# The last sum of the rotary embedding in a decoder's first attention: from GpSimd to VectorE

## The chip, the core and the metric

The kernel runs on one core of a Trainium2 chip. The metric is the device time of one execution in microseconds (us). All data are float32 unless said otherwise.

## What is computed

A decoder of four layers works on a stream x of shape (4, 256, 256). Each layer has three blocks (an attention, a cross block and a feed-forward block), and after each block comes x = layernorm(x + block(x)). The edit lies in the first block of layer 0, and the second block of layer 0 runs beside it. Cut to what matters:

```python
# layer 0, attention: 16 query heads of 128, one shared key and value head
q, k, v = x @ Wq, *split(x @ Wkv)
q, k = rope(q) * 128**-0.5, rope(k)   # rope(t) = t*cos + rotate_half(t)*sin
x = layernorm(x + softmax(causal(q @ k.T)) @ v @ Wout)

# layer 0, cross block: a selective scan over ctx (4, 256, 128), gated by x
u = silu(conv4(in_proj @ ctx))        # 256 channels
delta, Bm, Cm = softplus(...), ..., ...
for t in range(256):                  # 16 states per channel
    state = state * exp(delta[t] * A) + delta[t] * u[t] * Bm[t]
    y[t] = sum(state * Cm[t])
x = layernorm(x + (y + D * u) * silu(x))
```

rotate_half exchanges the two halves of a head's 128 entries and negates one of them. The remaining ten blocks are not touched.

## The kernel before

The twelve blocks are written one after the other. The instructions of each engine are put in order when the program is built: a scheduler with its own cost model arranges them, and each engine then works through its list strictly in that order, waiting at semaphores for the others. So an edit of one line can move others. Loads are issued from SP's queue.

**The attention** is `run_mqa`. Heads stand on the 128 partitions and tokens along the rows. `keys(h)` makes the keys of two batches at once (two calls), and `queries(n)`, n from 0 to 31, makes two heads of one batch: eight matmul instructions in the records into one PSUM tile of 128x512, and then the rotation. Every such tile goes through `rotated` (line 254), 34 calls in all:

- line 259, VectorE: out = ps * cos, 128x512, with ps in PSUM (in the profile qT<-ps or kT<-ps)
- lines 260 and 261, VectorE: the two halves of t = swapped ps * sin, 64x512 each (ropet<-ps); the sign is in the table
- line 262, GpSimd: out = out + t, 128x512, everything in SBUF (qT<-qT,ropet or kT<-kT,ropet)

All VectorE tensor_tensor operations go through the helper `tt` and carry line 111 in the profile; GpSimd's go through `ptt` and carry line 123, and activations of ScalarE line 126. Groups are therefore told apart by the names of their tiles. t has two buffers (`wk`), the queries have six (`qp`), and the PSUM tile of the projections (`pm`) has one.

The loop at line 368 runs n from 0 to 31. Step n covers half of the rows of one batch for four heads, with 128 keys (n even) or 256 (n odd): `shares(n)` inverts the row sums (VectorE's reciprocal of sm) and scales the exponentials p (ScalarE); `scores(n + 1)` makes the next scores (TensorE), their negated maxima nm (VectorE, two reductions) and exponentials (ScalarE); `queries(n + 4)` prepares four steps ahead; `turn(n)` transposes p; `sums(n)` and `output(n - 1)` are the products with v and Wout.

**The scan beside it.** `K.scans.beside(2)` (line 378) adds two of 64 scan steps (4 batches, 16 states) to each step of the loop. One step of the scan (`Scans._steps`):

```python
t = wk.tile([P, 2, L], F32, name="bc", tag="bc")          # Bm and Cm of this state, by DMA
K.act(dA[:, c, 1:L], delta[...], AF.Exp, scale=negA[...])  # ScalarE, twice
K.tt(s, du[:, :, lo : lo + L], again(t[:, 0, :], DC), MUL) # VectorE, s<-du,bc
nc.vector.tensor_tensor_scan(out=s, data0=dA, data1=s)     # VectorE, s<-dA,s (cut)
K.tt(s, s, again(t[:, 1, :], DC), MUL)                     # VectorE, s<-s,bc
```

All three are 128x512. TensorE adds up the states (ssmps<-s,idz). dA has three buffers and s four. Before the first step the scan has a preparation that runs beside the first steps of the attention: four products tap = tap * in on GpSimd, convolution matmuls in four groups of eight (ssmps<-ctxp,tap) into a single PSUM bank, each group moved to u by ScalarE, then Silu over all of u, the projection xd (copied by ScalarE, written to DRAM and read back as bc), delta by Exp and Ln, and du = delta * u on GpSimd.

GpSimd also adds epsilon and takes the power -0.5 for each layer norm (rstd), and multiplies the gate of the second block (gate<-gate,u, four times).

Of the kernel before, what the change touches and what calls it, by code (L numbers as in the profile page):

```python
# [29 lines left out]
ADD, SUB, MUL, MAX, MIN = ALU.add, ALU.subtract, ALU.mult, ALU.max, ALU.min  # L30
# [175 lines left out]
def again(ap, n):  # L206

    return ap.unsqueeze(1).to_broadcast([ap.shape[0], n, ap.shape[1]])
# [23 lines left out]
def run_mqa(K, w, more):  # L232
    nc, tc = K.nc, K.tc
    with ExitStack() as ctx:
# [11 lines left out]
            out=mask, in_=mask, compare_op=ALU.is_ge, fill=NEG, base=0, pattern=[[-1, P]], channel_multiplier=1  # L246
# [7 lines left out]
        def rotated(out, ps, cos, sin):  # L254

            v = lambda ap: ap.rearrange("p (b l) -> p b l", l=L)
            half = lambda ap, lo: again(ap[lo : lo + 64, :], 2)
            t = wk.tile([P, 512], F32, name="ropet")
            K.tt(v(out), v(ps), again(cos, 2), MUL)
            K.tt(v(t[0:64, :]), v(ps[64:128, :]), half(sin, 64), MUL)  # L260
            K.tt(v(t[64:128, :]), v(ps[0:64, :]), half(sin, 0), MUL)
            K.ptt(out, out, t, ADD)

        kT = one.tile([P, B * L], F32, name="kT")
        vt = one.tile([P, NT, P], F32, name="vt")
# [1 line left out]
        def keys(h):  # L267
            ps = (psc if h == 0 else pm).tile([P, 512], F32, name="ps", tag="sc" if h == 0 else "mm")
            for c in range(DC):
                K.mm(ps, w["kv"][:, c, 0:P], K.xT[:, c, 512 * h : 512 * h + 512], c == 0, c == DC - 1)  # L270
            rotated(kT[:, 512 * h : 512 * h + 512], ps, rope[:, 2, :], rope[:, 3, :])
# [9 lines left out]
        def queries(n):  # L281

            b = n // 8
            ps = pm.tile([P, 2, L], F32, name="ps", tag="mm")
            for j in range(2):
                h = n % 8 * 2 + j
                for c in range(DC):
                    K.mm(ps[:, j, :], w["q"][:, c, h * P : (h + 1) * P], K.xT[:, c, b * L : (b + 1) * L], c == 0, c == DC - 1)
            q = qp.tile([P, 2, L], F32, name="qT")
            rotated(q.rearrange("p j l -> p (j l)"), ps.rearrange("p j l -> p (j l)"), rope[:, 0, :], rope[:, 1, :])  # L290
            qT[n] = q
# [2148 lines left out]
```

## Time and profile before

| | |
|---|---|
| Median of 3 runs | 2475.49 us (2472.06 to 2479.26) |
| Profiled execution, its time | 2469.83 us |
| Its span in the profile | 2468.1 us |
| Mean granted TensorE clock | 0.948 |
| Busy: TensorE, VectorE, ScalarE, GpSimd | 2265.7, 1457.9, 801.0, 383.2 us |
| The 32 sums qT<-qT,ropet on GpSimd | 50.2 us, mean 1569 ns |
| The 2 sums kT<-kT,ropet on GpSimd | 3.0 us, mean 1516 ns |
| The 32 products qT<-ps on VectorE | 657 to 693 ns each |
| The 68 products ropet<-ps on VectorE | 683 to 694 ns each |

The first rotation starts at 10.5 us and the last one ends at 339.3 us, so everything that the edit touches lies in the first seventh of the span. In the rows of groups, a name such as s<-du,bc is what is written and what is read; then come the shapes, the count, the busy time in us and the mean in ns, and after the second bar the idle time of the engine just before. In rows ordered by time, the first two numbers are start and duration. Rows of waits give the total, the count and the longest wait, in us. The granted clock is the share of full speed at which TensorE was allowed to run. Spans on GpSimd are rough in such profiles.

### The profile page before, as it was taken

Reading aid. Unit: us, or ns where it says so; the run is one execution under the profiler, and the core shown is the slowest. Engines: PE = TensorE matmul, PEld = TensorE weight load, DVE = VectorE, ACT = ScalarE, POOL = GpSimd, SP = SyncE. Lnnn points to the kernel's source line nnn. Section 1 sums busy time; section 2 is a strip of 40 time slices with the busy share of each in tenths; the row PEclk is TensorE's granted clock in tenths of the full one; section 3 lists DMA queues with packets and bytes.
Section 4 is the critical chain, followed back from the end, with each engine's and each line's share of the span. In section 5 each row is a group of like instructions: output and inputs, shape, how many; then the busy total and the mean of one; then the engine's idle time right before and its main releaser. Section 6 shows DMA issues by size and latency. Waiting matters only on the chain. (4 is left out here: it accounts for less than half of the span.)

```text
span 2468.1 us, 28762 instructions
## 1 busy us (share of the span) xinstructions
PE 2265.7 (92%) x10624; PEld 1521.6 (62%) x10624; DVE 1457.9 (59%) x2920; ACT 801.0 (32%) x1781; POOL 383.2 (16%) x521
## 2 busy tenths in 40 slices
PE   8889998659986999899999999999999988899997
PEld 4466664325434655536888888888776543476774
DVE  3799983788875211280455444444556677774566
ACT  4567663523441111162211111111122243343434
POOL 2221214132330322200011000100210002100001
PEclk9999997778887999999999999999988899999999
DMA  6222221322213544220222112110100002100000
GB/s 201 60 60 59 53 52 35 70 48 50 52 39 101 164 131 127 78 77 9 73 82 87 45 46 73 45 63 31 46 22 1 20 18 71 41 1 1 1 1 18
DMA packets 132836, 138.99 MB, mean 56 GB/s; under 512 B 13876, under 2 KB 120726, under 8 KB 130904
## 3 DMA queue, kind: packets, MB, share of 16 engines
q1 hardware_dynamic: 132696, 137.16, 19.1%
q8 instruction: 84, 1.38, 0.2%
q14 instruction: 56, 0.46, 0.1%
HBM read 134.27 MB, written 2.85 MB: 56 GB/s over the span
## 5 line engine op out<-in xcount | busy, mean ns | idle before, releaser
L132 PE MATMUL ps<-xw,xcT 128*128 128x256 f32 (+1 forms) x2304 | 518.9, 382 | 0.3 <-ACT YT L126 0.3
L132 PEld LDWEIGHTS ps<-xw,xcT 128*128 128x128 f32 x2304 | 430.8, 190 | 64.0 <-issue 1.9
L132 PE MATMUL sc<-kT,qT 32*128 32x256 f32 (+2 forms) x1024 | 239.1, 403 | 11.7 <-DVE qn L129 11.3
L132 PEld LDWEIGHTS sc<-kT,qT 128*128 128x128 f32 (+1 forms) x1024 | 151.7, 200 | 89.7 <-issue 53.5
L111 DVE TENSOR_TENSOR xp<-ps,xb 128x256 f32<-128x256 f32 x96 | 40.4, 421 | 229.7 <-PE ps L132 229.6
L521 DVE TENSOR_TENSOR_SCAN s<-dA,s 128x512 f32<-128x512 f32 x128 | 160.2, 1266 | 15.4 <-POOL s L123 15.3
L132 PE MATMUL ssmps<-s,idz 128*128 128x512 f32 x256 | 142.8, 664 | 24.9 <-DVE s L111 24.0
L126 ACT ACTIVATE dA<-delta,negA 128x255 f32<-128x255 f32 x256 | 116.6, 501 | 133.7 <-DVE s L521 133.6
L126 ACT ACTIVATE p<-sc,nm 128x256 f32<-128x256 f32 (+1 forms) x256 | 111.8, 444 | 101.5 <-DVE nm L129 96.3
L111 DVE TENSOR_TENSOR hT<-u,a 128x512 f32<-128x512 f32 x48 | 33.2, 691 | 186.1 <-PE u L132 186.1
L132 PE MATMUL o<-pT,vt 128*128 128x256 f32 (+1 forms) x352 | 115.0, 449 | 15.5 <-ACT pT L332 15.1
L126 ACT ACTIVATE sq<-xp 128x1024 f32<-128x1024 f32 x24 | 25.4, 1057 | 314.3 <-DVE xp L111 314.3
L129 DVE TENSOR_REDUCE qn<-sc 128x2 f32<-128x480 f32 (+1 forms) x192 | 87.1, 506 | 40.1 <-PE sc L132 38.4
L123 POOL TENSOR_TENSOR xp<-xp,rn 128x128 f32<-128x128 f32 x96 | 35.2, 403 | 476.9 <-DVE rn L1408 476.9
L126 ACT ACTIVATE e<-sT 128x512 f32<-128x512 f32 x128 | 70.2, 590 | 107.7 <-PE sT L132 106.5
L129 DVE TENSOR_REDUCE nm<-sc 128x2 f32<-128x512 f32 (+1 forms) x128 | 76.7, 612 | 45.8 <-PE sc L132 45.5
L1476 DVE TENSOR_TENSOR_SCAN dec<-xT,idz 128x256 f32<-128x256 f32 (+1 forms) x192 | 89.8, 536 | 22.1 <-DMA xT<-ad 22.1
L132 PE MATMUL sT<-q,kT 32*128 32x256 f32 (+1 forms) x384 | 98.7, 501 | 1.7 <-ACT e L126 1.5
L169 POOL TENSOR_SCALAR rstd<-mv 128x2 f32<-128x2 f32 x48 | 11.7, 245 | 555.1 <-DVE mv L161 545.2
L126 ACT ACTIVATE a<-g 128x512 f32<-128x512 f32 x48 | 28.7, 597 | 206.9 <-PE g L132 206.8
L132 PE MATMUL g<-xT,wj 128*128 128x512 f32 x192 | 92.1, 603 | 0.7 <-ACT rows L100 0.7
L123 POOL TENSOR_TENSOR hT<-hT,sel 128x512 f32<-128x512 f32 x48 | 60.7, 1267 | 202.1 <-DVE hT L111 101.1
(504 smaller groups left out, 4133.2 us busy)
## 6 DMA issues: line engine op xcount, KB each, us to landing
bc<-bcd SPq DMA_DIRECT2D x128, 256.0 KB, 4.6
xw<-in_l2a_xw_dram SPq DMA_DIRECT2D x24, 768.0 KB, 4.9
xT<-ad SPq DMA_DIRECT2D x12, 1024.0 KB, 4.6
wj<-in_l1f_gate_dram SPq DMA_DIRECT2D x48, 128.0 KB, 2.5
wj<-in_l1f_up_dram SPq DMA_DIRECT2D x48, 128.0 KB, 2.8
wj<-in_l1f_down_dram SPq DMA_DIRECT2D x48, 128.0 KB, 2.9
sel<-cwd SPq DMA_DIRECT2D x32, 192.0 KB, 3.1
sel<-cwd SPq DMA_DIRECT2D x32, 128.0 KB, 3.2
```

The costliest lines, as they stand in the source:

```text
L111: self.nc.vector.tensor_tensor(out=out, in0=a, in1=b, op=op)
L123: self.nc.gpsimd.tensor_tensor(out=out, in0=a, in1=b, op=op)
L126: self.nc.scalar.activation(out, in_, func, **kw)
L129: self.nc.vector.tensor_reduce(out=out, in_=in_, axis=AX.X, op=op, **kw)
L132: self.nc.tensor.matmul(out, lhsT=lhsT, rhs=rhs, start=start, stop=stop)
L169: self.nc.gpsimd.tensor_scalar(out=out, in0=in_, scalar1=add, scalar2=None, op0=ADD)
L521: nc.vector.tensor_tensor_scan(out=s.rearrange("p c l -> p (c l)"), data0=dA.rearrange("p c l -> p (c l)"), data1=s.rearrange("p c l -> p ...
L1476: nc.vector.tensor_tensor_scan(out=dec[:, k, h, :], data0=ap[:, h, at(bb, k, j) : at(bb, k, 2)], data1=K.idz[:, 0 : (2 - j) * P], initial=0.0,
```

## The change

The fourth operation of the rotation is issued on VectorE instead of GpSimd. Its operands and its place in the source are the same; 34 instructions of 128x512 change their engine.

```diff
@@ rotated(out, ps, cos, sin)
             K.tt(v(out), v(ps), again(cos, 2), MUL)
             K.tt(v(t[0:64, :]), v(ps[64:128, :]), half(sin, 64), MUL)
             K.tt(v(t[64:128, :]), v(ps[0:64, :]), half(sin, 0), MUL)
-            K.ptt(out, out, t, ADD)
+            K.tt(out, out, t, ADD)
```

In the built program the order of the instructions changes on VectorE, ScalarE, TensorE and GpSimd within the first attention; behind it, it agrees with the order before. The order of the DMA issues on SP's queue is the same.

## The prediction

> **What bounds the kernel now.** I read the slices of the span first, for the stage in which the edited line runs: the first attention, from the start to about 370 us, with the first state-space scan beside it.
>
> ```profile
> DVE  3799983788875211280455444444556677774566
> POOL 2221214132330322200011000100210002100001
> ```
>
> One digit is 61.7 us. VectorE's second to sixth digits, 7 9 9 9 8, cover 62 to 370 us: it is full there, while GpSimd never passes a quarter. Busy times by stretch say where that begins and ends:
>
> ```profile
> core 0: us, PE busy (x) PEld busy (x) DVE busy (x) ACT busy (x) POOL busy (x), PEclk, DMA share, GB/s
> 0.00:85.00 85.00, 71.79 (x263) 43.29 (x264) 32.76 (x53) 42.55 (x97) 21.57 (x34) 0.98 0.50 158
> 85.00:100.00 15.00, 9.24 (x28) 4.79 (x27) 14.69 (x19) 6.49 (x14) 0.24 (x1) 0.97 0.26 71
> 100.00:340.00 240.00, 217.63 (x941) 152.25 (x940) 232.58 (x352) 158.64 (x457) 51.20 (x40) 0.98 0.23 58
> ```
>
> From 85 us, where the scan's first multiply runs, to 340 us VectorE is 97% busy. TensorE shows 91%, but that counts matmuls that stand in the pipeline: eight 256-column query matmuls take 1.89 us of path and are booked at 389 ns each, 3.1 us. VectorE's own waits in 100 to 340 us come to 5.8 us:
>
> ```profile
> DVE x L117 <- POOL rstd L123: 4.8, 6, 0.8
> DVE qT L111 <- PE ps L132: 1.0, 1, 1.0
> ```
>
> So in these 255 us the end is set by the sum of VectorE's instructions, and what an instruction occupies counts even when no wait is shown. Last, VectorE's groups with shapes kept apart, and the order in time (start, duration, engine, line, operation) of VectorE and GpSimd round one of the 34 rotations:
>
> ```profile
> L521 DVE TENSOR_TENSOR_SCAN s<-dA,s 128x512 f32<-128x512 f32 x51 | 64.5, 1290 | 0.0
> L111 DVE TENSOR_TENSOR s<-du,bc 128x512 f32<-128x512 f32 x52 | 53.7, 1066 | 0.1
> L111 DVE TENSOR_TENSOR s<-s,bc 128x512 f32<-128x512 f32 x50 | 32.5, 675 | 0.3
> ```
>
> ```profile
> 203.78 1.26 DVE L111 TENSOR_TENSOR s<-s,bc 128x512 f32<-128x512 f32 x2
> ...
> 208.34 0.18 DVE L320 RECIPROCAL sm<-sm 128x4 f32<-128x4 f32 x1
> 208.44 2.34 DVE L111 TENSOR_TENSOR s<-du,bc 128x512 f32<-128x512 f32 x2
> 210.70 2.33 DVE L521 TENSOR_TENSOR_SCAN s<-dA,s 128x512 f32<-128x512 f32 x2
> ```
>
> ```profile
> 208.46 1.77 POOL L123 TENSOR_TENSOR qT<-qT,ropet 128x512 f32<-128x512 f32 x1 [7.40 <-PE ps L330]
> ```
>
> Two multiplies of the same shape, both with two inputs in SBUF, take 1.26 us at 203.78 (the next starts 1.19 us later) and 2.34 us at 208.44, while GpSimd's rotation sum runs from 208.46 to 210.23. The trace has the pair as 0.66 and 1.76 us: the second stands still until GpSimd is done. GpSimd pays too: its sum takes 1.26 us alone and 1.77 us here. The mean of 1066 against 675 ns is this stall. GpSimd's "idle" 80% hides that each of its sums is paid for by VectorE.
>
> **The change, part by part.**
>
> *Removed: the stall.* Of the 34 sums, 25 run after 100 us (one of the keys, 24 of queries). For each I compared the VectorE instruction under it with the same instruction undisturbed (s<-du,bc 0.67 us, scan 1.21): 18 cost 1.00 to 1.10 us on a multiply, four 1.08 to 1.09 on a scan (2.29 us), three 0.38 to 0.41, because two instructions on PSUM filled most of the sum's time. Together 25.0 us, all on the path. The nine sums before 100 us lie under rotations and reductions that read PSUM and stall nothing (ropet 0.69 us with and without GpSimd).
>
> *A rule behind this row.* The Trainium skill ("SBUF — State Buffer", Who interferes with whom) says that a VectorE instruction with two SBUF inputs and a GpSimd instruction that reads SBUF exclude each other, the later one blocking until the earlier is through. By the rule alone each sum could cost 1.26 us, 31.5 in all; the trace has 25.0, since sums partly lie under work that doesn't contend. I take 25.0. The rule that speaks against the change is in "Perfetto Trace Analysis", Optimizing Scalar/DVE Operations: when VectorE is saturated, giving work to another engine, even GpSimd, may pay (it adds that between these two it might not). Taken plainly, 25 sums on a full engine are 15.0 us lost, 2490 us; by the row the same sums are 25.0 us lost where they are now, so the difference is a gain of 10.0.
>
> *Added: 34 sums on VectorE.* Nearest row: s<-s,bc, same shape and two SBUF inputs, 0.60 us from start to start. 25 x 0.60 = 15.0 us on the path. The upper bound is the full duration, 0.69 us (17.3), if the next instruction has to wait for the result; the built order of the changed program puts another instruction between nearly always. The nine early sums fall where VectorE is busy 39% and cost nothing: cover is idle time of up to 10.5 us before its reductions; without it, 9 x 0.60 = 5.4.
>
> *Moved: the order on VectorE.* The order is the scheduler's, so I read the built program. The two scan steps of an iteration, paired now (multiply twice, scan twice, multiply twice), are mostly interleaved with the sum and with the next maxima. One thing costs: the reciprocal of the row sums waits for ScalarE's exponentials. Now the query rotation, 2.07 us, stands between the second maximum and the reciprocal; in four iterations of the saturated stage there is only one 0.60 us multiply there. ScalarE needs 1.2 to 1.35 us after the second maximum (206.24 to 207.6), so each waits some 0.7 us: 2.8 us. Behind the waiting reciprocal stand the next rotation and multiply, and ScalarE's scaling waits for it. Bounds: 0, if ScalarE catches up, to 5, if ScalarE has scan exponentials queued ahead.
>
> *Moved: GpSimd's queue.* The four products tap<-tap,in, which open the scan's preparation, stand behind the fifth rotation sum and run at 32.14 us; their rows have landed by about 29. In the changed program they are the first tensor work on GpSimd. TensorE's first group of convolution matmuls starts at 33.18, behind scores that wait for that sum; in the new order it stands after three query matmuls, which start at 30.91 for another reason (PSUM is free when the rotation at 29.44 has ended), so it can start at about 31.6. ScalarE's eviction of that group, now at 37.18 behind four exponentials and two scalings, comes after two exponentials, at about 33.9. The next groups follow at some 4.3 us (eight matmuls of 0.43 and an eviction of 0.69), the last eviction at about 46.6 instead of 50.59, since five transposes and an output matmul fewer stand before it. A 0.6 us copy now stands ahead of the Silu over the whole preparation, which so starts at about 49.3 instead of 52.59. From the first xd copy (56.75) on, the orders agree, so the scan, which starts at 85.27 and makes VectorE the bound, starts 3.3 us sooner. VectorE idles before it, so this is gain: 3.3 us (bounds 0 and 4). The order of DMA issues does not change.
>
> *Rest of GpSimd in the stage.* It keeps the gate products (1.26 us) and the small roots. Three gate products lie under rotations that read PSUM; they do so in the new order. If they met a multiply, 3 x 1.1 = 3.3 us would come back; I take 0.
>
> *The sum.* -25.0 + 15.0 + 2.8 - 3.3 = -10.5 us. The profiled execution took 2469.83 us with a span of 2468.1; it becomes 2459.3. It is 5.66 us under the median of the runs, 2475.49, and I carry the same difference over: 2465.0 us. Nothing after the attention is edited, and the order there agrees. What is next to be late is VectorE still: it loses some 4% of its 255 us, ScalarE is 66% busy.
>
> **The rivals.**
>
> *Order rival, slower.* In the saturated stage VectorE depends on a ring: reciprocal, ScalarE's scaling, transposes, output sums, next scores, maxima, exponentials, reciprocal. With 256 keys the scores end 5.2 us after the reciprocal (199.18 to 204.46). VectorE now fills 5.8 us before the first maximum (stalled multiplies among them). In the new order it gets there after 4.7 us and to the second maximum after 5.3: it just fits, with nothing to spare. If VectorE waits there 1.0 us in each of 25 iterations, the place being the maxima and reciprocals, that is +25 - 10.5: 2490 us. It decides from 0.42 us per iteration (10.5 / 25). For it: the four short gaps above. Against: 20 of the 24 gaps before a reciprocal stay at 2.0 us or more, and VectorE has scan work from other iterations in between.
>
> *Half-gain rival, no difference.* The scan doesn't start sooner (another wait in its preparation takes over) and sums cost their full duration: -25.0 + 17.3 + 2.8 = -4.9: 2470.6 us. For it: ScalarE is in order and crowded from 31 to 57 us.
>
> *The gain is lost later.* After 370 us TensorE's granted clock is 0.83, then 0.62 (420 to 460 us); a stage that starts sooner might be granted less. The profile can't price it; if half goes, 2470.
>
> *Offloading pays, the change does not do what it says.* If the slow multiplies had another cause than GpSimd, all 15.0 us would be loss: 2490. Against: all 25 lengthened instructions lie under GpSimd's sum and none elsewhere.
>
> **How the numbers follow.** Forecast 0.66 (its own range 2458 to 2468), half gain or later loss 0.22, order rival 0.09, other cause 0.03. The range takes in the half gain, all favourable bounds (-25 + 15 - 4 = -14) and the 3.5 us by which the runs of before lie to either side of their median: 2456 to 2475. 0.3%, 7.4 us, is about what a measurement of this kernel tells from no change; forecast and half gain spread over that bound: faster 0.70, within 0.19, slower 0.11.
>
> **What would show it.** In the changed profile: s<-du,bc at some 0.67 us in the mean, no scan of 2.3 us; qT<-qT,ropet 32 times on VectorE at 0.67 to 0.69 us; GpSimd busy about 53 us less; the scan's first multiply at about 82 us; VectorE's waits in the stage up by 3 us, on ScalarE before the reciprocal. Wrong if VectorE's busy time in the stage falls and its idle time takes that over, or if multiplies stay long.

## The result and the profile after

The kernel with the sum on VectorE took 2465.89 us in the median of 10 runs (2457.00 to 2475.32), the kernel before beside it 2474.69 (10 runs, 2467.87 to 2479.79): ratio 0.9962, 95% interval 0.9944 to 0.9979. Timed once more with the experiments, it took 2469.46 (14 runs) beside 2472.51 (43 runs): 0.9989 (0.9967 to 1.0011).

The two intervals just overlap, and the granted clock tells why they lie so far apart. Over the 162 runs of the kernel before that stand beside the experiments, the time falls by 1.63 us for each 0.001 of mean granted clock (correlation -0.95; once this is taken out, the standard deviation falls from 7.0 to 2.3 us). The first 10 runs of the changed kernel had a mean clock of 0.9458, the later 14 one of 0.9426. Brought to a clock of 0.945 by that slope, the kernel before takes 2472.1 us, and the changed one 5.0 (standard error 0.8) and 4.2 (0.7) us less: 4.6 (0.5) over all 24. So the forecast of 2465.0 met the first median, but of the 8.8 us between the first two medians the change itself accounts for some 5, 0.2% and not the 10.5 us forecast. The rest fits the clock, though the clock of the ten runs of before in that first comparison is not on record.

The profiled execution took 2465.41 us (span 2463.6, clock 0.947). First come the slices of the span, VectorE and GpSimd:

```profile
DVE  4799982888866121380455444444556677774566
POOL 0000014132330322200100001100210002100001
```

VectorE is still at 9 from the third digit to the fifth, with GpSimd nearly empty beside it. Next come the busy times of 100 to 340 us, in the columns as before:

```profile
100.00:340.00 240.00, 223.97 (x968) 157.26 (x969) 230.43 (x387) 163.64 (x473) 9.40 (x15) 0.98 0.27 60
```

In the same 240 us VectorE does 387 instructions instead of 352 in slightly less busy time. These are some of its groups in that stretch, shapes kept apart:

```profile
L521 DVE TENSOR_TENSOR_SCAN s<-dA,s 128x512 f32<-128x512 f32 x53 | 64.1, 1216 | 0.1
L111 DVE TENSOR_TENSOR s<-s,bc 128x512 f32<-128x512 f32 x54 | 36.5, 685 | 0.4
L111 DVE TENSOR_TENSOR s<-du,bc 128x512 f32<-128x512 f32 x53 | 35.4, 672 | 0.2
...
L111 DVE TENSOR_TENSOR qT<-qT,ropet 128x512 f32<-128x512 f32 x24 | 16.4, 684 | 0.0
```

The first multiply of the scan is back to 672 ns (from 1066), the scan to 1216 (from 1290), and the sums stand in their place at 684. Here is one step in order of time, VectorE's rows:

```profile
206.13 0.18 DVE L320 RECIPROCAL sm<-sm 128x4 f32<-128x4 f32 x1
206.22 0.66 DVE L111 TENSOR_TENSOR s<-du,bc 128x512 f32<-128x512 f32 x1
206.80 0.69 DVE L111 TENSOR_TENSOR qT<-qT,ropet 128x512 f32<-128x512 f32 x1
207.40 1.22 DVE L521 TENSOR_TENSOR_SCAN s<-dA,s 128x512 f32<-128x512 f32 x1
```

Behind the reciprocal, where two multiplies took 2.34 us, a multiply and the sum now take 1.27, each its plain time. The waits of VectorE in the stretch have one new row, the reciprocal for ScalarE's exponentials:

```profile
DVE x L117 <- POOL rstd L123: 5.0, 6, 0.8
DVE sm L320 <- ACT p L126: 2.9, 4, 0.7
```

Marks in time show where the gain lies (starts in us; "stretch" is the time from the scan's first multiply to the last qT<-ps):

| | before | after |
|---|---|---|
| first product tap<-tap,in on GpSimd | 32.14 | 26.52 |
| first convolution matmul | 33.18 | 33.61 |
| first eviction to u | 37.18 | 37.24 |
| Silu over u | 52.59 | 53.41 |
| the scan's first multiply | 85.27 | 86.80 |
| the last qT<-ps | 335.31 | 329.57 |
| stretch | 250.0 | 242.8 |
| the last s<-du,bc | 360.78 | 353.77 |

The stretch as one window, first before and then after, says what it is made of; VectorE's busy time is the third pair:

```profile
85.30:335.30 250.00, 221.87 (x945) 153.53 (x944) 242.61 (x364) 162.75 (x465) 49.43 (x39) 0.98 0.24 60
```

```profile
86.80:329.60 242.80, 222.66 (x947) 154.70 (x946) 233.36 (x389) 162.73 (x465) 9.40 (x15) 0.97 0.27 60
```

So the stretch beside the scan is 7.2 us shorter: VectorE is busy 9.25 us less and idle 2.05 us more. It ends before the sum of the last query and so holds 24 of the 25 late sums. From the first to the last s<-du,bc, between which all 25 lie, the time is 275.5 us before and 267.0 after. The scan itself starts 1.5 us later, not 3.3 sooner.

Behind the attention the lead of the changed profile is not constant. Compared at instructions of the same name, it grows from 7.0 us at the last s<-du,bc to some 8 us from 420 to 1260 us, and falls to 4.7 by 1320 us; at the end of the span it is 4.4. Where it falls, the changed profile alone has TensorE at a granted clock of 0.50, from 1285.6 to 1289.0 us. That explains 1.7 us of the fall at most; the rest stays open.

### The profile page after: what moved, and what is told of

It is laid out like the page before. It is cut to its first block, busy times and chain, and to the rows that moved or that the text cites. A ratio compares the mean times of both kernels' runs of the same rounds, so it can differ in the third digit from the quotient of the medians.

```text
span 2463.6 us, 28734 instructions
## 1 busy us (share of the span) xinstructions
PE 2268.2 (92%) x10624; PEld 1523.0 (62%) x10624; DVE 1451.5 (59%) x2954; ACT 801.6 (33%) x1781; POOL 331.3 (13%) x487
## 5 line engine op out<-in xcount | busy, mean ns | idle before, releaser
L521 DVE TENSOR_TENSOR_SCAN s<-dA,s 128x512 f32<-128x512 f32 x128 | 156.9, 1233 | 15.5 <-POOL s L123 15.4
L126 ACT ACTIVATE a<-g 128x512 f32<-128x512 f32 x48 | 28.7, 597 | 206.9 <-PE g L132 206.9
L132 PE MATMUL u<-xT,wj 128*128 128x512 f32 x192 | 91.1, 596 | 0.0
```

The costliest lines, as they stand in the source:

```text
L126: self.nc.scalar.activation(out, in_, func, **kw)
L132: self.nc.tensor.matmul(out, lhsT=lhsT, rhs=rhs, start=start, stop=stop)
L521: nc.vector.tensor_tensor_scan(out=s.rearrange("p c l -> p (c l)"), data0=dA.rearrange("p c l -> p (c l)"), data1=s.rearrange("p c l -> p ...
```

## The experiments

All edits are to the changed kernel; the diffs are cut to the lines that matter. The table has the plain comparison, and beside it the difference from the kernel before at the clock of 0.945 (standard errors 0.4 to 0.7 us, 0.8 for the first row) and the stretch as in the table above.

| | median us | ratio to before (95%) | at equal clock, us | stretch, us |
|---|---|---|---|---|
| changed kernel | 2465.89 | 0.9962 (0.9944 to 0.9979) | -5.0 | 242.8 |
| the same again (e14_after) | 2469.46 | 0.9989 (0.9967 to 1.0011) | -4.2 | 242.9 |
| e1_shadow | 2494.76 | 1.0093 (1.0060 to 1.0127) | +14.1 | 262.8 |
| e2_twice | 2483.83 | 1.0037 (1.0021 to 1.0053) | +9.1 | 256.2 |
| e3_late | 2466.25 | 0.9962 (0.9943 to 0.9982) | -5.9 | 242.8 |
| e7_early | 2476.39 | 1.0022 (1.0005 to 1.0040) | +1.6 | 250.0 |
| e5_timed | 2469.47 | 0.9982 (0.9967 to 0.9998) | -7.7 | 242.9 |
| e13_root | 2487.57 | 1.0061 (1.0035 to 1.0087) | +10.1 | 256.4 |
| e8_product | 2496.36 | 1.0113 (1.0082 to 1.0143) | +23.9 | 263.8 |
| e10_half | 2475.00 | 1.0010 (0.9990 to 1.0029) | +5.3 | 245.6 |
| e9_write | 2472.61 | 1.0016 (0.9997 to 1.0035) | +0.2 | 244.3 |
| e11_fill | 2465.95 | 0.9967 (0.9946 to 0.9987) | -4.3 | 242.8 |
| e9_copy | 2479.35 | 1.0021 (1.0000 to 1.0042) | +5.7 | 252.8 |

Most rows rest on 14 to 22 runs; the changed kernel has 10, e13_root 9, e8_product 6 and e1_shadow 5. The stretch comes from one profile each; for one kernel it repeats to 0.1 us (the first two rows), at different clocks.

**Is the stall GpSimd's doing?** e1_shadow leaves the VectorE sum where it is and adds a sum on GpSimd that nobody reads.

```diff
+            junk = wk.tile([P, 512], F32, name="junk"); K.ptt(junk, t, t, ADD)
             K.tt(out, out, t, ADD)
```

> The changed kernel, to which each of the 34 rotations adds a sum on GpSimd that nobody reads: ropet plus ropet, 128x512, from SBUF to SBUF, at the place where the old sum stood. The order of VectorE, ScalarE and TensorE is that of the changed kernel; GpSimd has its old load again. Theory of the stall (VectorE's instructions with two SBUF inputs stand still while GpSimd reads SBUF): 25 sums after 100 us cost some 1.0 us each, +25 us, so about 2491 us; the stretch from the scan's first multiply to the last query product is 25 us longer than in the changed kernel (242.8), and instructions of 1.7 to 2.3 us are back on VectorE, now also among its own rotation sums. Rival (the gain came from the new order, or from GpSimd's result being ready sooner, not from the memory access): within 3 us of the changed kernel, 2466 us.

Measured: 20.0 us more stretch than the changed kernel. Here is a step of it, ordered by time, VectorE and then GpSimd:

```profile
217.95 0.66 DVE L111 TENSOR_TENSOR s<-du,bc 128x512 f32<-128x512 f32 x1
218.53 1.53 DVE L111 TENSOR_TENSOR qT<-qT,ropet 128x512 f32<-128x512 f32 x1
```

```profile
217.97 1.54 POOL L123 TENSOR_TENSOR junk<-ropet 128x512 f32<-128x512 f32 x1 [8.07 <-DVE ropet L111]
```

VectorE's second instruction takes 1.53 instead of 0.69 us; it stands still until GpSimd's sum ends at 219.51. Nobody waits for that sum: VectorE's waits in the stretch are those of the changed kernel (rstd 5.0, du 3.2, the exponentials 2.9). So the loss is the stall alone, and the theory stands; the rival in which the slow multiplies have another cause falls. The price of one sum, mostly 0.84 to 0.87 us, is smaller than the 1.09 of before, because this sum, of a tile with itself, is shorter. Where it starts ahead of VectorE's multiply it takes 1.04 us, while the old sum took 1.26 alone:

```profile
177.05 1.04 POOL L123 TENSOR_TENSOR junk<-ropet 128x512 f32<-128x512 f32 x1 [10.85 <-DVE ropet L111]
```

**What does a sum on VectorE cost?** e2_twice makes the sum twice there, the first time into an unread tile.

```diff
+            junk = wk.tile([P, 512], F32, name="junk"); K.tt(junk, out, t, ADD)
             K.tt(out, out, t, ADD)
```

> The changed kernel with each rotation sum made twice on VectorE (the first into a tile that nobody reads). Theory that VectorE's sum of instructions sets the stage: 25 more sums at 0.60 us, +15 us, 2481 us; the nine early ones shift the scan's first multiply (86.8 us) by up to 3 us more, since the early rotations turned out to be on the path, so up to 2484. Rival (the stage is held by TensorE or by the ring of scores and exponentials, VectorE's time has slack): under +5 us, 2466 to 2471 us.

Measured: the stretch grows by 13.4 us, 0.56 for each of the 24 sums in it, and the time at equal clock by 13.7. VectorE is busy 15.5 us more there (248.89 of 256.2 us) and idle 2.1 us less, since the second sum fills the wait before the reciprocal (0.1 us idle instead of 3.1). That is 0.65 us for one sum, so the price of 0.60 on the path lies between the two and holds, and the rival in which VectorE's time has slack falls.

**Early and late sums apart.** e3_late gives the first nine sums back to GpSimd, e7_early the other 25.

```diff
@@ e3_late
-            K.tt(out, out, t, ADD)
+            early.append(0); (K.ptt if len(early) < 10 else K.tt)(out, out, t, ADD)
@@ e7_early
-            K.tt(out, out, t, ADD)
+            early.append(0); (K.tt if len(early) < 10 else K.ptt)(out, out, t, ADD)
```

> Only the 25 late rotation sums are on VectorE; the nine that come before the scan starts stay on GpSimd. Theory of two terms (late sums gain, early ones cost since a key sum on VectorE delays the rotation behind it, by which TensorE waits for its PSUM tile): the scan's first multiply comes at about 85.3 us as in the kernel before, not at 86.8, the stretch from there to the last query product stays at 243 us, in all 1.5 us under the changed kernel, 2464 us. Rival (the late start in the changed profile was chance of the granted clock or of a transfer): the first multiply stays at 86 to 87 us.

> The complement of the mixed version: the nine sums before the scan go to VectorE, the 25 beside the scan stay on GpSimd. Theory (the whole gain lies in the stall of the late sums, and the early sums on VectorE cost a later start): the scan's first multiply at 86.8 us as in the changed kernel, 1.5 later than before; from there to the last query product 250 us as before; about 2474, that is before + 1.5. Rival (the early sums on VectorE are part of the gain): under 2471.

Measured: e3_late starts the scan at 85.49 and has the stretch of the changed kernel; e7_early starts it at 86.10 and has the stretch of before, and is 1.6 us (standard error 0.6) slower than before at equal clock. So the whole gain is in the late 25 sums, and the early nine on VectorE cost about a microsecond. That they "cost nothing" was wrong, and so was the sooner start. The start of the scan alone would be weak evidence, since it moves with the clock: e14_after, the changed kernel again, starts it at 88.44, with a mean clock of 0.96 in the first 85 us against 0.98 in the profile of the changed kernel above. At 0.98 the scan starts at 85.2 to 85.5 us where the early sums are on GpSimd (before, e3_late, e10_half), and at 86.1 to 86.9 where they are on VectorE (the changed kernel, e7_early, e11_fill).

**Can GpSimd keep the sums if they are timed?** e5_timed leaves the early sums on GpSimd and holds each late one until the next step's first maximum is done, where VectorE turns to PSUM. The hold is a GpSimd instruction of 280 ns that reads nm and rewrites a column of t.

```diff
+        def timed(late, z): [(nc.gpsimd.tensor_scalar(out=t[:, 0:1], in0=z, scalar1=0.0, scalar2=t[:, 0:1], op0=MUL, op1=ADD), K.ptt(out, out, t, ADD)) for out, t in late]; late.clear()
...
-            K.tt(out, out, t, ADD)
+            early.append(0); (late.append((out, t)) if len(early) > 10 else (K.ptt if len(early) < 10 else K.tt)(out, out, t, ADD))
...
-                K.reduce(nm[:, two], sc[:, :, 0:ns], MAX, negate=True)
+                K.reduce(nm[:, two], sc[:, :, 0:ns], MAX, negate=True); timed(late, nm[:, 0:1]) if jj == 0 else None
```

> The nine early sums and 23 or so late query sums are on GpSimd again, but each late one is held back until the next step's first maximum is there, by a GpSimd instruction on one column that reads this maximum times zero. From there VectorE works on PSUM for some 2.7 us (second maximum, three products of the next rotation), and GpSimd needs 1.5. Theory (only VectorE instructions with two inputs in SBUF stand still, those that read PSUM don't): neither the stall nor the sum is on VectorE's path, so 0.60 us per late sum, 14 us, under the changed kernel, and 1.5 us for the early ones: about 2451 us, no s<-du,bc above 0.8 us. Rival A (any GpSimd work costs VectorE about its time): as before, 2475 us. Rival B (the next bound, TensorE with some 8.6 us of matmuls per step, or the ring of scores and exponentials, holds the stage near the changed 9.7 us per step): 2460 to 2466 us, VectorE idle in the stage.

Measured: the stretch is 242.9, no shorter than with the sums on VectorE, though the stall is nearly gone (s<-du,bc 674 ns, the scan 1265, GpSimd's sum 1284). Here is its stretch as one window, to be compared with that of the changed kernel above:

```profile
87.40:330.30 242.90, 221.82 (x945) 155.54 (x944) 224.58 (x365) 163.48 (x465) 48.27 (x61) 0.96 0.26 61
```

VectorE works 8.8 us less and idles 8.9 us more, as rival B said. Its waits in this kernel's stretch say for what:

```profile
DVE x L117 <- POOL rstd L123: 10.0, 6, 2.0
DVE qT L111 <- PE ps L132: 4.6, 6, 1.0
DVE s L111 <- POOL du L123: 3.2, 1, 3.2
DVE nm L129 <- PE sc L132: 2.1, 7, 0.4
```

Against the changed kernel, rstd is up by 5.0, the query projections and scores by 6.7, and the wait before the reciprocal (2.9) is gone: 8.8. The 5.0 is a queue. In five of the six steps with a layer norm GpSimd makes the second half of the norm's root behind the held sum. These are its instructions in one such step, and the VectorE scan beside them:

```profile
152.83 1.22 POOL L169 TENSOR_SCALAR rstd<-mv 128x2 f32<-128x2 f32 x1
154.01 1.26 POOL L123 TENSOR_TENSOR qT<-qT,ropet 128x512 f32<-128x512 f32 x1
155.23 0.71 POOL L123 TENSOR_TENSOR rstd<-rstd,power 128x2 f32<-128x2 f32 x1
```

```profile
152.81 1.21 DVE L521 TENSOR_TENSOR_SCAN s<-dA,s 128x512 f32<-128x512 f32 x1
```

The first half of the root, rstd<-mv, takes 1.22 us here and 0.22 in the changed kernel. It starts just behind the scan and ends with it: this time it is GpSimd that stands still.

At equal clock this version has the lowest time of all, 3.1 us (standard error 0.7) under the changed kernel and 1.8 (0.8) under e3_late, which like it has the early sums on GpSimd. By the plain ratios that doesn't show, and its stretch is no shorter, so where those 1.8 us would come from is not shown.

e13_root tries to take the root out of that queue: in steps with a layer norm, the sum waits for rstd instead of nm.

```diff
@@ against e5_timed
-                K.reduce(nm[:, two], sc[:, :, 0:ns], MAX, negate=True); timed(late, nm[:, 0:1]) if jj == 0 else None
+                K.reduce(nm[:, two], sc[:, :, 0:ns], MAX, negate=True); timed(late, nm[:, 0:1]) if jj == 0 and (n < 9 or n % 8 not in (1, 3)) else None
...
-            sums(n)
+            sums(n); (timed(late[:1], K.held), late.pop(0)) if n > 7 and n % 8 == 0 and late else None
...
-                gate_pair(K, wk, y, n // 8 - 1)
+                gate_pair(K, wk, y, n // 8 - 1); (timed(late[:1], K.held), late.pop(0)) if late else None
```

> The version with GpSimd sums held until VectorE reads PSUM, altered where a layer norm falls into the step: there the sum is held until the norm's root is done, so that the root need not queue behind it (the built order still has a sum ahead of the root's second half in some of them). Theory (VectorE's waits for rstd, 10.0 us there against 5.0, are the root behind the sum): 2 to 5 us under that version, stretch 238 to 241 us, about 2465 or less. Rival (the ring through TensorE holds it): no change, 2469, and the waits move to sc and ps.

Measured: 13.5 us more stretch. TensorE has a wait in the stretch that it had not in e5_timed:

```profile
PE sc L132 <- POOL qT L123: 20.1, 5, 5.5
```

The queries came so late that TensorE's scores waited for them, and VectorE's wait for rstd stayed at 9.1. Neither theory was tested: the edit made a wait of its own.

**Is VectorE alone the bound?** e8_product has no query sum at all; scores are accumulated on TensorE as q*k + t*k, and t takes a tile from the query pool. e10_half does that for every second query tile and has the early sums on GpSimd.

```diff
-                    K.mm(sc[:, j, 0:ns], q[:, j, t * P : (t + 1) * P], kT[:, b * L : b * L + ns], False, j == 1)
+                    [K.mm(sc[:, j, 0:ns], h[:, j, t * P : (t + 1) * P], kT[:, b * L : b * L + ns], False, j == 1 and h is r) for h in (q, r)]
```

> The query sum is left out on every engine: the scores are accumulated on TensorE as q*k + t*k, so 24 of the late VectorE sums go and TensorE gets four more matmul instructions of 128 or 256 keys in each step. If only VectorE's sum of instructions counts: 24 x 0.60 = 14.4 us under the changed kernel, 2451. If TensorE is the next bound (its path grows from 8.6 to some 9.9 us per step, against VectorE's 9.7 before and 9.1 now): about 2471, VectorE idle before its maxima (waits on sc and ps of 10 us or more in the stage).

> Early nine sums on GpSimd; of the late ones every second query sum stays on VectorE, and for the others the scores are accumulated on TensorE as q*k + t*k. VectorE loses 12 x 0.60 = 7.2 us of the stage, TensorE gains some 0.65 us per step (9.25 against VectorE's 9.4). If VectorE's sum still decides: 2466.3 - 7.2 = 2459. If the ring through TensorE decides: 2465 or more, with VectorE's waits on sc and ps grown by 5 us or more.

Measured: with all sums gone the stretch grows by 21.0 us, and with half of them gone by 2.8. Here is e8_product's stretch as one window, and VectorE's waits in it:

```profile
84.50:348.30 263.80, 251.36 (x1157) 184.98 (x1156) 224.76 (x371) 166.53 (x471) 9.37 (x15) 0.99 0.23 56
```

```profile
DVE nm L129 <- PE sc L132: 16.1, 17, 1.3
DVE qT L111 <- PE ps L132: 10.6, 11, 1.0
DVE sm L320 <- ACT p L126: 6.2, 5, 1.2
```

VectorE idles 39 us here, mostly behind TensorE, which idles only 12.4 (263.8 less the 251.36 of the first pair). TensorE's busy time is 28.7 us longer than in the changed kernel: 1.15 for each of 25 steps, where I had expected 1.3. In the changed kernel TensorE is busy for 222.66 us of the stretch and VectorE for 233.36. As a rough estimate, since the ends of matmuls are modelled, TensorE is next in line by 10.7 us, 0.4 per step. This is e10_half's stretch:

```profile
85.20:330.90 245.70, 230.35 (x1031) 164.57 (x1030) 228.18 (x378) 163.47 (x465) 11.83 (x15) 0.99 0.26 59
```

With 12 sums fewer, VectorE is busy 5.2 us less than in the changed kernel and idle 8.1 us more (5.2 us behind the query projections, 4.4 behind the exponentials), and TensorE idles 15.4 us. Neither is full; that the ring of their waits then sets the time is the likely reading, which no run tests by itself. In any case less work on VectorE brought nothing. In both kernels q and t share the six query buffers, but this doesn't show as the limit: from the ninth query on, a rotation starts 17 to 31 us before the first maximum that needs it in e8_product, and 14 to 29 in the changed kernel.

e10_half is 11 us slower than e3_late at equal clock, while its last s<-du,bc starts 4.9 us later (357.37 against 352.44); where the rest arises was not found.

**What on GpSimd stalls VectorE?** e9_write replaces the unread GpSimd sum of e1_shadow by a fill with zeros, e11_fill fills t itself behind its last use, and e9_copy makes the unread sum an unread copy.

```diff
@@ e9_write
+            junk = wk.tile([P, 512], F32, name="junk"); nc.gpsimd.memset(junk, 0.0)
             K.tt(out, out, t, ADD)
@@ e11_fill
             K.tt(out, out, t, ADD)
+            nc.gpsimd.memset(t, 0.0)
@@ e9_copy
+            junk = wk.tile([P, 512], F32, name="junk"); nc.gpsimd.tensor_copy(junk, t)
             K.tt(out, out, t, ADD)
```

> As the kernel with an unread GpSimd sum beside each VectorE sum, but the GpSimd instruction only fills the tile with zeros and reads nothing. If the stall comes from GpSimd's reading of SBUF: as the changed kernel, 2466, s<-du,bc 0.67 us. If any GpSimd access to SBUF of that size stalls VectorE: up to 2491, s<-du,bc 0.75 us and scans of 2.3 us.

> The fill that reads nothing, this time tied to its place: behind each VectorE sum GpSimd fills ropet with zeros, after its last use, so the 25 late fills lie beside the scan's work. A fill took 0.47 us in the back-to-back series of the last batch. If only GpSimd's reading of SBUF stalls VectorE's multiplies and scans: as the changed kernel, 2466, stretch 243 us. If writing does it too: some 0.35 to 0.45 us for each, 9 to 11 us, 2476, stretch 252 us.

> The unread GpSimd sum of the first batch turned into an unread copy, one input instead of two, on the same tiles, between the rotation's last product and the VectorE sum. If the stall is the GpSimd instruction's whole time: its duration times 25 less what lies under PSUM work, for a copy of 0.6 to 0.9 us some 10 to 17 us, about 2480. If two inputs on GpSimd are needed: as the changed kernel, 2466.

e9_write missed its aim: nothing held the fills, and all 34 ran back to back at the start. What they did there is under the surprises below. e11_fill and e9_copy are tied to their place. Here is the same step in each, VectorE and then GpSimd, first e11_fill, then e9_copy:

```profile
206.92 0.69 DVE L111 TENSOR_TENSOR qT<-qT,ropet 128x512 f32<-128x512 f32 x1
207.52 1.22 DVE L521 TENSOR_TENSOR_SCAN s<-dA,s 128x512 f32<-128x512 f32 x1
```

```profile
207.72 0.53 POOL L262 MEMSET ropet<- 128x512 f32 x1 [8.25 <-DVE qT L111]
```

```profile
212.52 0.66 DVE L111 TENSOR_TENSOR s<-du,bc 128x512 f32<-128x512 f32 x1
213.09 1.09 DVE L111 TENSOR_TENSOR qT<-qT,ropet 128x512 f32<-128x512 f32 x1
```

```profile
212.52 1.13 POOL L262 COPY junk<-ropet 128x512 f32<-128x512 f32 x1 [8.06 <-DVE ropet L111]
```

The fill from 207.72 to 208.25 lies within a scan that takes its plain 1.22 us, and so do 15 more; s<-du,bc has 673 ns in the mean and the stretch is the changed kernel's. The copy ends at 213.65, and VectorE's sum takes 1.09 instead of 0.69 us: 10.0 us of stretch, 0.4 for each of the 24 in it. So one GpSimd input from SBUF is enough for the stall, and writing alone causes none on these instructions. This is what the Trainium skill says ("SBUF — State Buffer", Who interferes with whom): it is GpSimd's reading that collides with two SBUF inputs on VectorE.

**The changed kernel again.** e14_after is without an edit.

> The changed kernel itself, unaltered, in the same batch as the next three, since it had been timed 10 times only. From the marks in the profiles (1.5 us later start of the scan, 7.2 us shorter stretch behind it) it should stand 5.7 us under the kernel before when both are compared at one granted clock, and about 2466 by the plain median.

Measured: 4.2 us (standard error 0.7) under before at equal clock; 5.7 was expected. The plain median, 2469.46, is 3.5 us above the expected 2466, at a clock lower by 0.0032 than in the first runs.

## Why the prediction was right, and where not

- *The stall removed and the sums added, -25.0 + 15.0.* Right in mechanism and in size. VectorE's busy time in the stretch fell by 9.25 us, where 24 of the 25 sums should give 9.6. With the wait below, the forecast gives -7.2 for all 25 sums, and from the first to the last s<-du,bc the time fell by 8.5; that the stretch with 24 fell by exactly 7.2 is chance. e1_shadow and e2_twice price the two parts singly.
- *Reciprocals wait 2.8 us for the exponentials.* Right in place, number and size: four, 2.9 us in all.
- *Nine early sums cost nothing.* Wrong by about a microsecond: e3_late starts the scan 1.3 us sooner than the changed kernel. The cover named, idle time before the reductions, is there. But the key's sum stands ahead of the next rotation's products in VectorE's order, and that rotation frees the only projection tile, for which TensorE's next group of query matmuls waits. Here are the first two groups, before, in e7_early and in the changed kernel, and the key's sum in e7_early:

```profile
10.23 1.94 PE L132 MATMUL ps<-xT,w_q 128*128 128x256 f32 x8
14.85 1.97 PE L132 MATMUL ps<-xT,w_q 128*128 128x256 f32 x8 [1.93 <-DVE ropet L111]
```

```profile
10.25 2.25 PE L132 MATMUL ps<-xT,w_q 128*128 128x256 f32 x8
15.46 1.97 PE L132 MATMUL ps<-xT,w_q 128*128 128x256 f32 x8 [2.53 <-DVE ropet L111]
```

```profile
10.37 2.92 PE L132 MATMUL ps<-xT,w_q 128*128 128x256 f32 x8
16.16 1.62 PE L132 MATMUL ps<-xT,w_q 128*128 128x256 f32 x3 [2.66 <-DVE ropet L111]
```

```profile
13.23 0.68 DVE L111 TENSOR_TENSOR kT<-kT,ropet 128x512 f32<-128x512 f32 x1
```

The sum of 0.68 us moves the second group from 14.85 to 15.46. The further 0.7 us in the changed profile are not the sum's: there the first group takes 2.92 us instead of 1.94, and the first product of its rotation, qT<-ps, comes at 13.32 instead of 12.62. The key's sum alone was not tried; the nine were only moved together.
- *The scan starts 3.3 us sooner.* This is the step that failed. The tap products did leave the queue (26.52). But the query matmuls that were to start at 30.91 "for another reason" depend on the chain just named and start at 32.31 (in e7_early at 31.62). And I let the first eviction follow 2.3 us after the start of the convolution group, though its eight matmuls take 3.60 us, a figure that the profile of before has, as these rows of before and after show:

```profile
33.18 3.60 PE L132 MATMUL ssmps<-ctxp,tap 128*128 128x512 f32 x8
```

```profile
33.61 3.60 PE L132 MATMUL ssmps<-ctxp,tap 128*128 128x512 f32 x8
```

The scan starts 1.5 us late, and 0.8 in e7_early, where the first qT<-ps comes at 12.62 (12.60 before); the term is off by 4.1 to 4.8. The first half of the half-gain rival (the scan doesn't start sooner) is what happened, with a shorter stretch than that rival had; its total of -4.9 us is the nearest to the measured -4.6.
- *The order rival.* It didn't occur: VectorE has no wait on sc or ps in the stretch. But "what is next to be late is VectorE still" was too simple, and "TensorE shows 91%, but that counts matmuls that stand in the pipeline" was misread: the busy time of a window counts overlapping records once (eight query matmuls of some 0.38 us each are 1.97 us in the rows above, not 3.1), so the 91% is not swollen by counting them twice. e8_product and e10_half show TensorE close behind VectorE.
- *The gain is lost later by the clock.* The runs don't show it: over its 24 runs the changed kernel has a mean clock of 0.9440, the kernel before 0.9443 over 162. But two sets of runs of one kernel differ in mean clock by 0.0032, worth 5 us. The clock scatters by as much as this change is worth, and the changed kernel's first ten runs had the higher one.
- *The sum.* By the profile's marks it is -7.2 + 1.5 = -5.7 us (-7.0 with the last sum, at the last s<-du,bc), at equal clock -4.6 (0.5), where -10.5 was forecast. That 2465.0 was met is luck to a good part: from the forecast's base of 2475.49 a gain of 4.6 leads to 2470.9, and the other 5 us are of the size that the clock scatters by.

## What to carry to other kernels

An engine at 20% busy can still cost: price what its instructions do to the neighbour that they collide with, not only what they take themselves. When work is moved onto a full engine, cost it from the row of the same shape there, and then ask what is next in line: here TensorE was busy only 10.7 us less than VectorE. And when a change is worth 0.2%, look at how the time follows the granted clock before reading a ratio.

## What the runs showed of the hardware that was not expected

In e9_write 34 GpSimd fills of 128x512, with one more fill between them, ran back to back from 2.35 to 18.5 us. These are GpSimd's row of the first 13 and two VectorE copies of 128x128 that change the type, ordered by time:

```profile
2.35 6.12 POOL L262 MEMSET junk<- 128x512 f32 x13
```

```profile
2.06 16.55 DVE L64 CAST identb<-idz 128x128 bf16<-128x128 f32 x1 [2.06 <-POOL idz masks.py:199]
2.30 16.37 DVE L251 CAST maskb<-mask 128x128 bf16<-128x128 f32 x1
```

The copies end when the series of fills ends: they stood still for 16 us, through the whole series and not for one fill. So fills, which leave VectorE's sums and scans alone, do stop its copies. The section of the skill named above has copies and casts among the instructions that can contend with GpSimd for the shared ports, the loser waiting for the whole of the other's instruction; here the loser waited for 34 of them. Whether these copies were in the two-port mode that it speaks of, no run shows. The scan then started at 95.71, 8.9 us after the changed kernel's; the timed runs show 4.8 us of that at equal clock, and where the rest comes back was not settled.

A VectorE instruction with one input can stand still beside GpSimd's sum too, against what the prediction says of the nine early sums. Here is a small scaling in the kernel before, beside the GpSimd sum that runs from 19.02 to 20.28 us, and the same scaling in the changed kernel, where no such sum runs:

```profile
19.32 1.01 DVE L115 TENSOR_SCALAR negA<-negA 128x32 f32<-128x32 f32 x1
```

```profile
22.16 0.17 DVE L115 TENSOR_SCALAR negA<-negA 128x32 f32<-128x32 f32 x1
```

It took 1.01 us in e3_late as well, which has this sum on GpSimd, and 0.17 in e7_early, which has not. Nobody waited for it, and VectorE was idle for 1.09 us behind it in the kernel before, so it cost nothing.
